# One y tile per x tile, a reordered whitening chain, packing by TensorE in pairs, and a reordered start in a convolution and whitening kernel

## The chip, the cores and the metric

The kernel runs on one core of one Trainium2 chip. Its engines are named as in the profile: PE (TensorE, with PEld for its weight loads), DVE (VectorE), ACT (ScalarE), POOL (GpSimd) and SP (SyncE, which only issues DMAs). The metric is the device time of one execution in microseconds; lower is better.

## The reference

Two layers, all in float32. Layer 0 is a separable long convolution of x (4 images, 64 channels, 256 x 256) with a filter that a small network of sines computes; layer 1 whitens the 64 channels. Cut to what matters:

```python
# layer 0, for each filter (X: rows, Y: columns)
h = sin(freq * (z @ w1 + b1)); h = sin(freq * (h @ w2 + b2)); h = sin(freq * (h @ w3 + b3))
h = (h @ wo) * exp(-t * abs(deltas))             # 256 taps for each channel
k[c] = outer(hx[:, c], hy[:, c])
y = irfft2(rfft2(x) * rfft2(k) / 512)[:256, :256]  # causal 2-D convolution
x = y + x * bias[:, None, None]
# layer 1
x1 = transpose(x, (1, 0, 2, 3)).reshape(64, -1)
x1_s = x1[:, ::9]                                 # every 9th pixel
xc = x1 - mean(x1_s)
cov = x1_s @ x1_s.T / n + 0.01 * eye(64)
normA = norm(cov); Y = cov / normA; Z = eye(64)
for _ in range(5):                                # Newton-Schulz
    T = 0.5 * (3 * I - Z @ Y); Y = Y @ T; Z = T @ Z
out = (Z / sqrt(normA)) @ xc
```

## The kernel before, in words

The kernel has four parts in time.

*The start* (lines 85 to 175). The filter network's weights (`zw`, `cols`, `wbd`, `decay`) and two tables (`mask`, `bias`) are loaded, five of the six on ACT's queue; three layers of product, Identity, range reduction on DVE and Sin give `taps`, which go to HBM (`g_d`) and come back as Toeplitz tiles, each row shifted by one. `busy` issues products of zeros as filler for TensorE between the layers. A float32 product is issued as two passes, so `busy(8)` shows as 16 matmuls.

*The convolution.* There are 32 steps, each one image `n` and one block `g` of 8 channels; each step is worked off in four groups of two channels (`c` = 0, 2, 4, 6). In `group`, TensorE multiplies one pair by the first filter (`job1`, from the x tile) and, interleaved with it, the pair of two groups earlier by the second filter (`job2`). ACT copies the first result to `o1`; DVE adds `x * bias` to the second result and writes y (line 398). `store` sends y to HBM, to `y_d`. The first two groups and the last two run alone, in `half_group`. Once a step's y is whole, `pack_ops` adds nine `copy_predicated` on DVE that pick every 9th pixel into `samp`; `pack` runs about three of them in each group. For the last half of the last step the picking is done by TensorE (`pack_by_pe`, one product for each of nine phases and two halves with the matrices `pick`). `covariance(n)` multiplies the samples of an image once its last step is done.

*The chain* (lines 473 to 562). From the covariance follow the norm, five Newton-Schulz iterations of small 64 x 64 products, the scaled matrix `W` and the vector `shift`.

*The whitening.* y is read back in 32 pieces of 2 MB (`load_y`), multiplied by `W` (line 580), shifted on ACT and DVE (lines 585 and 588) in place, and written out by DMAs that GpSimd issues (line 593).

In memory, the pool `big` holds two x tiles (`in`) and two y tiles (`out`). After the convolution, x, y, filter, sample and two extra tiles become homes for pieces of y: `homes` lists 13, in the order in which they are taken, and piece 13 takes the first home again after its store. The order of work is written out by hand and kept on every engine (`manual_schedule`): SyncE issues x loads, y stores, filter loads (`blocks`) and reads of y in program order, and a DMA that waits holds up those behind it. `early` says after which step and group how many pieces of y are already asked for; the rest of the 13 follow after the last covariance. SyncE's DMAs use eight completion semaphores in turn, so each also waits for the eighth before it.

Of the kernel before, what the change touches and what calls it, by code (L numbers as in the profile page):

```python
# [48 lines left out]
CG = 8  # L49
# [16 lines left out]
def conv_whiten_kernel(ctx: ExitStack, tc: tile.TileContext, a: dict, out: bass.AP):  # L66
# [4 lines left out]
    big = ctx.enter_context(tc.tile_pool(name="big", bufs=2))  # L71
# [13 lines left out]
    scratch = big.tile([P, 16, L], F32, tag="out", name="scratch")  # L85
# [4 lines left out]
    nc.scalar.dma_start(out=cols, in_=a["cols"])  # L90
    wbd = scratch[:, 0:2, :].rearrange("p a w -> p (a w)")[:, 0 : 3 * P]
    nc.scalar.dma_start(out=wbd, in_=a["wbd"])
    decay = scratch[:, 15, :]
    nc.scalar.dma_start(out=decay, in_=a["decay"])
    mask = const.tile([P, NB, H2, STEP], I32, tag="mask", name="mask")
    nc.scalar.dma_start(out=mask, in_=a["mask"])
    bias = const.tile([P, C], F32, tag="bias", name="bias")
    nc.scalar.dma_start(out=bias, in_=a["bias"].partition_broadcast(P))
# [11 lines left out]
    x_tiles = [big.tile([P, CG, H2, L], F32, tag="in", name=f"x{u}") for u in range(2)]  # L110
    for c in range(0, CG, 2):
        load_x(x_tiles[0], *steps[0], c)

# [22 lines left out]
    bf = const.tile([P, 3], F32, tag="bf", name="bf")  # L136

    nc.vector.memset(bf[:, 0:1], 0.0)
    nc.scalar.activation(bf[:, 1:2], bf[:, 0:1], AF.Sin)
# [12 lines left out]
    for i in range(3):  # L152
        for u in range(2):
            pm = psA.tile([P, P], F32, tag="psA", name=f"pm{i}_{u}")
            nc.tensor.matmul(pm, lhsT=wt, rhs=hs[u], start=True, stop=True)  # L155
            half = slice(u * P, (u + 1) * P)
            arg, k, nxt = (scratch[:, 2 + 3 * i + v, half] for v in range(3))
            nc.scalar.activation(arg, pm, AF.Identity, bias=bf[:, i : i + 1], scale=freq)
            nc.vector.tensor_scalar(k, arg, 1.0 / (2.0 * math.pi), MAGIC, ALU.mult, ALU.add)
            nc.vector.tensor_scalar(k, k, MAGIC, None, ALU.subtract)  # L160
            for part in (TP1, TP2):
                nc.vector.scalar_tensor_tensor(arg, k, -part, arg, ALU.mult, ALU.add)  # L162
            nc.vector.tensor_scalar(arg, arg, 3.1415925, -3.1415925, ALU.min, ALU.max)
            nc.scalar.activation(nxt, arg, AF.Sin)
            hs[u] = nxt
        wt = wbd[:, i * P : (i + 1) * P]
        busy((8, 10, 9)[i])
# [92 lines left out]
    def half_group(item, which):  # L260

        g, n, c, xt, yt, o1s = item
# [11 lines left out]
        for m in range(H2):  # L274
            for u in range(2):
                ps = jobs[u][0][m]
                if which == 0:
                    copy = nc.vector.tensor_copy if u else nc.scalar.copy
                    for to, fr in ((slice(0, HP), slice(HP, P)), (slice(HP, P), slice(0, HP))):
                        copy(o1s[u][to, m], ps[fr])  # L280
                else:
                    ch = g * CG + c + u
                    nc.vector.scalar_tensor_tensor(  # L283
                        yt[:, c + u, m], xt[:, c + u, m], bias[:, ch : ch + 1], ps,
                        ALU.mult, ALU.add,
                    )

    def pack_by_pe(g, n, yt, cs):
# [15 lines left out]
        nc.vector.tensor_copy(dst[:, 1], pk[:, 1].rearrange("p c j -> p j c"))  # L304
# [15 lines left out]
    def covariance(n):  # L320
# [20 lines left out]
        {"t": (tpool, "toep"), "s": (spool, "samp"), "i": (big, "in"), "o": (big, "out"), "e": (epool, "extra")}[k]  # L341
        for k in "eetssitsoiots"
# [28 lines left out]
    early = {(26, 4): 1, (26, 6): 1, (27, 4): 1, (28, 2): 1, (29, 6): 1, (31, 4): 2, (31, 6): 1}  # L371
# [8 lines left out]
    def group(first, second):  # L380

        units = []
        g1, n1, c1, x1, _, o1s1 = first
        g2, n2, c2, x2, y2, o1s2 = second
# [7 lines left out]
        for u in range(2):  # L392
            o1 = o1pool.tile([P, H2, L], F32, tag="o1", name=f"o1_{g1}_{n1}_{c1 + u}")
            for to, fr in ((slice(0, HP), slice(HP, P)), (slice(HP, P), slice(0, HP))):
                nc.scalar.copy(o1[to], units[u][0][0][fr])  # L395
            o1s1.append(o1)
            ch = g2 * CG + c2 + u
            nc.vector.scalar_tensor_tensor(  # L398
                y2[:, c2 + u], x2[:, c2 + u], bias[:, ch : ch + 1], units[u][1][0],
                ALU.mult, ALU.add,  # L400
            )
# [4 lines left out]
    def store(second):  # L406
        g, n, c, _, yt, _ = second
# [7 lines left out]
        if last and c == CG // 2 - 2 or not last and c == CG - 2:  # L415
            todo.extend(pack_ops(g, n, yt, slice(0, c + 2)))

    engines = mybir.EngineType
    with tc.manual_schedule(
# [9 lines left out]
        for i, (g, n) in enumerate(steps):  # L429
            xt = x_tiles[i % 2]  # L430
            yt = big.tile([P, CG, H2, L], F32, tag="out", name=f"y_{g}_{n}")
            for c in range(0, CG, 2):
                item = (g, n, c, xt, yt, [])
# [7 lines left out]
                if i == 0 and c == 6:  # L441
# [3 lines left out]
                    twice = const.tile([C, 2, C], F32, tag="twice", name="twice")  # L445
                    for u in range(2):
                        nc.vector.tensor_copy(twice[:, u], ident[0:C, 0:C])

                j, cj = i - (c < 4), (c - 4) % CG
                if 0 <= j < len(steps) - 2:  # L450
                    load_x(x_tiles[j % 2], *steps[j + 2], cj)
# [8 lines left out]
        g, n, c, xt, yt, _ = pending[0]  # L460
# [6 lines left out]
        pack_by_pe(g, n, yt, slice(CG // 2, CG))  # L467
# [3 lines left out]


    spare = {}
    for i in range(2):
        t = o1pool.tile([P, H2 * L], F32, tag="o1", name=f"chain{i}")
        for j in range(5):
            spare[5 * i + j] = t[0:C, 72 * j + 72 : 72 * j + 72 + C]
    ones = spare[9]
    nc.gpsimd.memset(ones, 1.0)  # L479
    i15 = spare[8]  # L480
    nc.vector.tensor_scalar(i15, ident[0:C, 0:C], 1.5, None, ALU.mult)
    spots = {"A": [0], "sq": [1], "Y": [2, 3], "T": [4, 5], "Z": [6, 7], "Zs": [1]}

    columns = [t[0:C, 440 + k : 441 + k] for k in range(H2 * L - 440)]

    def column():
        return columns.pop()

    def matrix(tag):
        spots[tag].append(spots[tag].pop(0))  # L490
        return spare[spots[tag][-1]]

    def product(lhsT, rhs, name):
        p = psA.tile([lhsT.shape[1], rhs.shape[1]], F32, tag="psA", name=name)
        nc.tensor.matmul(p, lhsT=lhsT, rhs=rhs, start=True, stop=True)  # L495
        return p

    def keep(p, name, tag):
        t = matrix(tag)
        nc.vector.tensor_copy(t, p)  # L500
        return t


    pd = product(fold, cov, "pd")
    A = matrix("A")
    nc.vector.scalar_tensor_tensor(A, ident[0:C, 0:C], EPS, pd[:, 0:C], ALU.mult, ALU.add)
    mean = column()
    nc.scalar.copy(mean, pd[:, C : C + 1])

    def root(v, name):  # L510

        s0 = column()
        nc.scalar.activation(s0, v, AF.Sqrt)  # L513
        r = column()
        nc.vector.reciprocal(r, s0)
        s1 = column()
        nc.vector.scalar_tensor_tensor(s1, v, r, s0, ALU.mult, ALU.add)
        s2 = column()
        nc.vector.tensor_scalar(s2, s1, 0.5, None, ALU.mult)
        return s2  # L520

    sq = matrix("sq")
    nc.vector.tensor_tensor(sq, A, A, ALU.mult)
    rowsum = column()
    nc.vector.tensor_reduce(rowsum, sq, AX.X, ALU.add)
    ssq = column()
    nc.vector.tensor_copy(ssq, product(ones, rowsum, "pn"))
    norm = root(ssq, "norm")
    rnorm = column()
    nc.vector.reciprocal(rnorm, norm)  # L530

    Y = matrix("Y")
    nc.vector.tensor_scalar(Y, A, rnorm, None, ALU.mult)
    Z = None
    for it in range(N_ITER):
        ZY = Y if Z is None else product(Z, Y, f"ZY{it}")
        T = matrix("T")
        nc.vector.scalar_tensor_tensor(T, ZY, -0.5, i15, ALU.mult, ALU.add)
        if it < N_ITER - 1:
            nextY = product(Y, T, f"YT{it}")  # L540
        if Z is None:
            newZ = T
        else:
            newZ = matrix("Z")
            nc.scalar.copy(newZ, product(T, Z, f"TZ{it}"))
        if it < N_ITER - 1:
            Y = keep(nextY, f"Y{it + 1}", "Y")
        else:
            snorm = root(norm, "snorm")
            rsnorm = column()  # L550
            nc.vector.reciprocal(rsnorm, snorm)
        Z = newZ

    Zs = matrix("Zs")
    nc.vector.tensor_scalar(Zs, Z, rsnorm, None, ALU.mult)
    twice = twice.rearrange("p u c -> p (u c)")
    W = o1pool.tile([P, H2 * L], F32, tag="o1", name="W")[:, 0:C]
    nc.vector.tensor_copy(W, product(twice, Zs, "pw"))
    shift0 = column()
    nc.vector.tensor_scalar(shift0, product(Zs, mean, "pz"), -1.0, None, ALU.mult)  # L560
    shift = const.tile([P, 1], F32, tag="shift", name="shift")
    nc.vector.tensor_copy(shift, product(twice, shift0, "ps"))
# [91 lines left out]
```

## Time and profile before

| | us |
|---|---|
| median of 3 runs (lowest, highest) | 917.46 (916.84, 920.22) |
| the profiled execution, its own time | 916.79 |
| span of the profiled execution, first to last instruction | 914.9 |
| PE busy (share of the span) | 789.4 (86%) |
| DVE busy | 657.7 (72%) |
| ACT busy | 479.1 (52%) |
| first convolution matmul | 19.63 |
| end of the last Toeplitz product | 621.4 |
| first store of the result issued | 653.81 |

Times inside the profile count from the start of the span. Shares of busy time are averages over stages that have different limits. The granted clock of TensorE was 0.946 on average. `yi` are pieces of y read back, `y_d` is y in HBM, `ph` and `p` are results of Toeplitz products, `pk` of packing, `pc` of the covariance, `po` of the whitening.

### The profile page before, as it was taken

How to read it: one execution, taken by the hardware profiler on the slowest of the kernel's cores; microseconds unless marked ns; L12 is line 12 of the kernel's file. 1: busy time of each engine (PE TensorE's matmuls, PEld its weight loads, DVE VectorE, ACT ScalarE, POOL GpSimd, SP SyncE). 2: the span in 40 equal slices, each digit the busy share in tenths (PEclk: the TensorE clock that was granted, in tenths of full speed). 3: DMA queues.
4: the chain of work that ended last, by engine and by line, in shares of the span. 5: the costliest groups of instructions: out<-in, count | busy, mean ns of one | idle time of the engine just before them, and what ended most of it. 6: DMA issues, size and time to landing. Idle time of an engine off the chain costs nothing.

```text
span 914.9 us, 28251 instructions
## 1 busy us (share of the span) xinstructions
PE 789.4 (86%) x11876; PEld 633.3 (69%) x11876; DVE 657.7 (72%) x882; ACT 479.1 (52%) x791; POOL 31.8 (3%) x71
## 2 busy tenths in 40 slices
PE   8999999999999999999999999997877777765500
PEld 7999999999999999999999999996311111121100
DVE  3468776878687868786878666866699999986500
ACT  2545454545454545454545444540598888865400
POOL 3000000000000000000000000000110000000010
PEclk9999999999999999999999999998799999987655
DMA  4988788788788888888997897849999999999998
GB/s 155 295 264 262 247 262 265 232 269 260 249 263 262 248 256 264 258 253 275 285 275 227 310 378 289 300 139 406 422 418 426 428 429 429 430 430 427 433 433 333
DMA packets 117549, 285.59 MB, mean 312 GB/s; under 512 B 8973, under 2 KB 91312, under 8 KB 109744
## 3 DMA queue, kind: packets, MB, share of 16 engines
q1 hardware_dynamic: 110224, 216.09, 69.2%
q0 software_dynamic: 6336, 67.11, 17.3%
q8 instruction: 94, 1.54, 0.7%
q10 hardware_dynamic: 864, 0.60, 0.2%
q14 instruction: 31, 0.25, 0.1%
HBM read 149.35 MB, written 134.42 MB: 310 GB/s over the span
## 4 chain that ended last, share of the span: by engine, by line
PE 68%; issue 15%; DVE 14%; ACT 0%; DMA 0%; POOL 0%; POOLq 0%; DVEq 0%; ACTq 0%; SPq 0%
PE p L214 63%; DVE yi L588 12%; PE pc L326 2%; PE ph L246 1%; PE pk L294 1%; POOL out_dram L593 0%; DMA toep<-g_d 0%; DVE y L283 0%; PE busy L149 0%; PE po L580 0%; PE ZY L495 0%; PE YT L495 0%; PE pm L155 0%; DVE scratch L162 0%; ACT L513 0%
## 5 line engine op out<-in xcount | busy, mean ns | idle before, releaser
L214 PE MATMUL p<-toep,o 64*64 64x64 f32 (+3 forms) x5040 | 578.4, 284 | 0.0
L214 PE MATMUL p<-toep,x 64*64 64x64 f32 (+3 forms) x5040 | 578.3, 284 | 0.0
L214 PEld LDWEIGHTS p<-toep,x 64*128 64x128 f32 (+1 forms) x5040 | 534.2, 166 | 23.1
L214 PEld LDWEIGHTS p<-toep,o 64*128 64x128 f32 (+1 forms) x5040 | 535.4, 166 | 10.5 <-issue 0.2
L395 ACT COPY o<-p 64x512 f32<-64x512 f32 x504 | 292.4, 580 | 297.3 <-PE p L214 289.7
L312 DVE COPY_PREDICATED samp<-mask,y 128x448 f32<-128x448 int32 (+3 forms) x288 | 281.1, 976 | 6.6
L398 DVE SCALAR_TENSOR_TENSOR y<-x,bias,p 128x512 f32<-128x512 f32 x252 | 177.3, 744 | 138.4 <-PE p L214 130.2
L588 DVE TENSOR_SCALAR yi<-po,shift 64x512 f32<-64x512 f32 x256 | 192.1, 750 | 24.5 <-PE po L580 18.2
L580 PE MATMUL po<-yi,W 64*64 64x512 f32 x1024 | 153.2, 674 | 61.8 <-DVE yi L588 40.4
L585 ACT ACTIVATE yi<-po,shift 64x512 f32<-64x512 f32 x256 | 174.9, 683 | 43.7 <-PE po L580 36.7
L580 PEld LDWEIGHTS po<-yi,W 64*64 64x64 f32 x1024 | 36.8, 146 | 176.9 <-DVE yi L588 125.0
L593 POOL DMA_DIRECT2D out_dram<-yi x44 | 23.7, 538 | 263.5 <-DVE yi L588 100.6
L479 POOL MEMSET chain<- 64x64 f32 x1 | 0.1, 145 | 602.2 <-PE ph L246 602.2
L326 PEld LDWEIGHTS pc<-samp 128*64 128x64 f32 x464 | 14.4, 137 | 2.0 <-issue 1.2
L326 PE MATMUL pc<-samp 128*64 128x65 f32 x464 | 15.1, 223 | 0.5 <-ACT samp L303 0.4
L149 PE MATMUL busy<-idle 128*128 128x128 f32 x94 | 12.9, 301 | 0.0
L149 PEld LDWEIGHTS busy<-idle 128*128 128x128 f32 x94 | 12.4, 216 | 0.2 <-issue 0.2
L280 DVE COPY o<-ph 64x256 f32<-64x256 f32 x8 | 3.4, 422 | 9.1 <-PE ph L246 8.9
L294 PE MATMUL pk<-y,pick 128*128 128x112 f32 (+1 forms) x36 | 7.7, 389 | 2.5 <-DVE y L283 2.5
L334 DVE SCALAR_TENSOR_TENSOR cov<-pc,cov 128x65 f32<-128x65 f32 x4 | 0.9, 227 | 12.4 <-PE pc L326 12.4
L294 PEld LDWEIGHTS pk<-y,pick 128*128 128x128 f32 x36 | 7.2, 260 | 2.8 <-issue 2.7
L280 ACT COPY o<-ph 64x256 f32<-64x256 f32 x8 | 2.9, 367 | 10.0 <-DMA toep<-g_d 8.5
(81 smaller groups left out, 79.7 us busy)
## 6 DMA issues: line engine op xcount, KB each, us to landing
x<-in_x_dram SPq DMA_DIRECT2D x128, 512.0 KB, 5.3
y_d<-y SPq DMA_DIRECT2D x256, 256.0 KB, 3.5
yi<-y_d SPq DMA_DIRECT2D x32, 2048.0 KB, 15.7
out_dram<-yi POOLq DMA_DIRECT2D x28, 2048.0 KB, 44.6
out_dram<-yi POOLq DMA_DIRECT2D x16, 512.0 KB, 9.0
toep<-g_d SPq DMA_DIRECT2D x29, 256.0 KB, 6.2
toep<-g_d SPq DMA_DIRECT2D x29, 192.0 KB, 5.6
toep<-g_d SPq DMA_DIRECT2D x6, 128.0 KB, 3.1
```

The lines of the kernel that those rows point to most:

```text
L149: nc.tensor.matmul(p, lhsT=idle[:, 0:P], rhs=idle[:, P : 2 * P], start=True, stop=True)
L214: mm = nc.tensor.matmul(ps[q : q + w, m, HP * k : L], lhsT=src[parts, k // 2, m * P + q : m * P + q + w], rhs=t[parts, : stop : -1] if k e ...
L246: mm = nc.tensor.matmul(ps[m][:, HP * k : L], lhsT=src[parts, k // 2, m * P : (m + 1) * P], rhs=t[parts, : stop : -1] if k else t[parts, : ...
L294: nc.tensor.matmul(pk[:, b, :, 0:nj], lhsT=pick[:, (s - b) % STEP, :], rhs=yt[:, cs, b, s : s + STEP * (nj - 1) + 1 : STEP], start=(s == 0 ...
L312: nc.vector.copy_predicated(dst, m, src)
L326: nc.tensor.matmul(pc[half], lhsT=samp[n][:, b, j, 0:C], rhs=samp[n][:, b, j, :], start=(b == 0 and j < 2), stop=(b == H2 - 1 and j >= NJ ...
L395: nc.scalar.copy(o1[to], units[u][0][0][fr])
L398: nc.vector.scalar_tensor_tensor(y2[:, c2 + u], x2[:, c2 + u], bias[:, ch : ch + 1], units[u][1][0], ALU.mult, ALU.add,)
L580: nc.tensor.matmul(po[u][halves[k]], lhsT=W[halves[u]], rhs=yt[halves[u], cols[k]], start=True, stop=True,)
L585: nc.scalar.activation(yt[halves[0], cols[k]], po[0][halves[k]], AF.Identity, bias=shift[halves[k]])
L588: nc.vector.tensor_scalar(yt[halves[1], cols[k]], po[1][halves[k]], shift[halves[k]], None, ALU.add)
L593: nc.gpsimd.dma_start(out=o[:, end - part : end], in_=yt[:, end - part : end])
```

## The change

The convolution writes y into the x tile. The pools `in` and `out` of two tiles each become one pool of four x tiles; step i+2 is loaded into the tile of step i-2, at the same `c`. The filter network's scratch moves to an extra tile. `homes` and `early` change with it: of the first 13 pieces nine instead of eight are asked for inside the steps, pieces 5 and 6 in step 30 and step 31 at `c` = 2.

At the start, ACT issues one DMA (`cols`) and then runs the first Sin; `wbd`, `decay`, `mask` and `bias` go to SyncE's queue, between and behind the first x loads. The first filler is 5 products instead of 8. An activation with Sqrt runs in step 0.

`pack_by_pe` is called twice, for two channels each; in the first call ACT makes both copies. The chain becomes a function, `whitening`, inside the manual schedule: the first iterate is a polynomial of the covariance and its square and cube, which are multiplied while the norm is still computed; afterwards T is squared and M is multiplied by it (three rounds), the mean is carried as a 65th column of Z, the last T is written twice side by side so that one product gives `W` and `shift` for both halves, and the scaling comes last. `spin` issues products of the identity as filler.

```diff
-    big = ctx.enter_context(tc.tile_pool(name="big", bufs=2))
+    xpool = ctx.enter_context(tc.tile_pool(name="xpool", bufs=4))
...
-    scratch = big.tile([P, 16, L], F32, tag="out", name="scratch")
+    scratch = epool.tile([P, 16, L], F32, tag="extra", name="scratch")
...
     nc.scalar.dma_start(out=cols, in_=a["cols"])
+    bf = const.tile([P, 3], F32, tag="bf", name="bf")
+    nc.vector.memset(bf[:, 0:1], 0.0)
+    nc.scalar.activation(bf[:, 1:2], bf[:, 0:1], AF.Sin)
...
-    nc.scalar.dma_start(out=wbd, in_=a["wbd"])
+    nc.sync.dma_start(out=wbd, in_=a["wbd"])
...
     for c in range(0, CG, 2):
         load_x(x_tiles[0], *steps[0], c)
+        if c == 0:
+            nc.sync.dma_start(out=decay, in_=a["decay"])
+    nc.sync.dma_start(out=mask, in_=a["mask"])
+    nc.sync.dma_start(out=bias, in_=a["bias"].partition_broadcast(P))
...
-        busy((8, 10, 9)[i])
+        busy((5, 10, 9)[i])
...
-        nc.vector.tensor_copy(dst[:, 1], pk[:, 1].rearrange("p c j -> p j c"))
+        copy = nc.vector.tensor_copy if cs.stop == CG else nc.scalar.copy
+        copy(dst[:, 1], pk[:, 1].rearrange("p c j -> p j c"))
...
-        for k in "eetssitsoiots"
+        for k in "eetssiistiits"
...
-    early = {(26, 4): 1, (26, 6): 1, (27, 4): 1, (28, 2): 1, (29, 6): 1, (31, 4): 2, (31, 6): 1}
+    early = {
+        (26, 4): 1, (27, 0): 1, (27, 4): 1, (28, 0): 1, (29, 6): 1, (30, 2): 1, (31, 2): 1, (31, 4): 1, (31, 6): 1
+    }
...
-                y2[:, c2 + u], x2[:, c2 + u], bias[:, ch : ch + 1], units[u][1][0],
+                x2[:, c2 + u], x2[:, c2 + u], bias[:, ch : ch + 1], units[u][1][0],
...
-                j, cj = i - (c < 4), (c - 4) % CG
-                if 0 <= j < len(steps) - 2:
-                    load_x(x_tiles[j % 2], *steps[j + 2], cj)
+                    nc.scalar.activation(bf[:, 0:1], samp[0][:, 0, 0, C : C + 1], AF.Sqrt)
+                if i + 2 < len(steps):
+                    load_x(x_tiles[(i + 2) % 4], *steps[i + 2], c)
...
-        pack_by_pe(g, n, yt, slice(CG // 2, CG))
+        for lo in range(CG // 2, CG, 2):
+            pack_by_pe(g, n, yt, slice(lo, lo + 2))
         covariance(NB - 1)
         while len(loaded) < len(homes):
             load_next()
+        W, shift = whitening(i15, ones)
```

The new chain, with its filler (a placed tile is a piece of an `o1` buffer; `product` is as before):

```python
def spin(times):
    p = psA.tile([P, P], F32, tag="psA", name=f"spin{len(spins)}")
    for _ in range(times):
        nc.tensor.matmul(p, lhsT=ident, rhs=ident, start=True, stop=True)

def whitening(i15, ones):
    pd = product(fold, cov, "pd")
    nc.vector.scalar_tensor_tensor(A, ident[0:C, 0:C], EPS, pd[:, 0:C], ALU.mult, ALU.add)
    nc.vector.tensor_tensor(sq, A, A, ALU.mult)
    pa2 = product(A, A, "pa2")
    pn = product(ones, sq, "pn")
    ...
    nc.vector.tensor_reduce(ssq, pn, AX.X, ALU.add)
    nc.scalar.activation(s0, ssq, AF.Sqrt)
    ...
    pa3 = product(A2a, A, "pa3")
    spin(7)
    ...
    nc.vector.scalar_tensor_tensor(rn, r3, hm, h, ALU.mult, ALU.add)
    ...
    nc.vector.scalar_tensor_tensor(U, pa3, rn_c, A2b, ALU.mult, ALU.add)
    nc.vector.scalar_tensor_tensor(V, U, rn_c, A1b, ALU.mult, ALU.add)
    nc.vector.scalar_tensor_tensor(T, V, rn_c, one_i15, ALU.mult, ALU.add)
    nc.vector.tensor_scalar(M, V, rn_c, -2.0, ALU.mult, ALU.mult)
    ...
    for k in range(1, N_ITER - 1):
        pq = product(T, T, f"pq{k}")
        if before is not None:
            next_z(k - 1, before)
        spin(1)
        nc.vector.tensor_copy(Q, pq)
        pm = product(Q, M, f"pm_{k}")
        ...
    pw = product(T, Z, "pw")
    nc.vector.tensor_scalar(W, pw[:, 0:C], rs, None, ALU.mult)
    nc.scalar.activation(shift, pw[:, C : C + 1], AF.Copy, scale=nrs)
```

## The prediction

> **What bounds the kernel now.** I read the slices first: which engine is full in which stage.
>
> ```profile
> PE   8999999999999999999999999997877777765500
> DMA  4988788788788888888997897849999999999998
> GB/s 155 295 264 262 247 262 265 232 269 260 249 263 262 248 256 264 258 253 275 285 275 227 310 378 289 300 139 406 422 418 426 428 429 429 430 430 427 433 433 333
> ```
>
> A slice is 22.9 us. TensorE is full for 26 slices (the convolution); from the 28th on the DMA engines are, at 406 to 433 GB/s (whitening: y is read back, transformed, written out). Between them lies the 27th slice, at 139 GB/s. So I cut the turn finer, with the table of windows (busy time of PE, PEld, DVE, ACT, POOL, then granted clock, DMA share, GB/s):
>
> ```profile
> 600.00:606.00 6.00, 6.00 (x142) 5.47 (x138) 3.15 (x4) 2.33 (x5) 0.00 (x0) 1.00 0.50 168
> 606.00:610.00 4.00, 4.00 (x48) 3.72 (x48) 0.23 (x1) 0.00 (x0) 0.00 (x0) 1.00 0.02 4
> 610.00:613.00 3.00, 3.00 (x94) 2.92 (x94) 2.43 (x4) 2.31 (x4) 0.00 (x0) 1.00 0.07 21
> 620.00:650.00 30.00, 20.14 (x205) 17.07 (x206) 15.97 (x47) 2.94 (x9) 0.00 (x0) 0.75 1.02 412
> 775.00:905.00 130.00, 58.98 (x360) 16.24 (x358) 72.46 (x97) 62.87 (x92) 9.66 (x19) 0.72 1.01 429
> ```
>
> The DMA engines are nearly idle until 613 and full from there to the end, through the serial chain too (620 to 650). The end is therefore set by two things: when TensorE's stream lets y come free, and how many bytes are still to be moved at 613. Who asks for them is SyncE's timeline:
>
> ```profile
> 577.39 0.40 SPq L350 DMA_DIRECT2D yi<-y_d  x1
> ...
> 613.33 0.94 SPq L350 DMA_DIRECT2D yi<-y_d  x2
> ...
> 617.25 0.42 SPq L350 DMA_DIRECT2D yi<-y_d  x1
> ...
> 627.21 11.32 SPq L350 DMA_DIRECT2D yi<-y_d  x5
> ```
>
> Tile 4 of y is read back at 577; tiles 5 and 6 only at 613, tile 7 at 617, 8 to 12 from 627. Thirteen tiles have a home before a store frees one.
>
> **The start.** From the timeline:
>
> ```profile
> 2.62 0.73 ACTq L98 DMA_DIRECT2D bias<-in_bias_dram  x1
> 3.38 1.28 ACT L139 ACT_TABLE_LOAD   x1 [3.38 <-issue]
> 3.73 3.70 PE L149 MATMUL busy<-idle 128*128 128x128 f32 x16
> 5.23 0.81 ACT L158 ACTIVATE scratch<-pm,bf,cols 128x128 f32<-128x128 f32 x2 [0.35 <-issue]
> 7.61 0.95 PE L155 MATMUL pm<-scratch 128*128 128x128 f32 x4 [0.19 <-ACT scratch L164]
> 19.63 6.41 PE L246 MATMUL ph<-toep,x 64*128 64x256 f32 x64 [0.32 <-DMA toep<-g_d]
> ```
>
> ACT issues five DMAs before it loads Sin's table at 3.38, and everything up to the first convolution matmul (19.63) hangs on the chain behind it. With one DMA ahead (0.74 to 1.14) the load ends at about 2.45, bf follows when cols lands (0.74 + 2.0 us), and the first Identity waits for pm, about 3.3 instead of 5.23: 1.9 us. The filler of layer 1 becomes 5 products, 10 passes: 3.70/16 = 0.231 us each, from 3.73 to 6.04. Layer 2's product would be ready at 7.61 - 1.9 = 5.7 and waits for that filler: 1.6 us remain. Layer 2's filler keeps its 20 passes, which took 2.40 us (0.12 each) from 8.40. [...] The granted clock column says 1.00 here, but passes of 0.231 and then 0.12 us show two speeds. By the row, those passes start at 6.8 mostly fast and cost 0.2; [...]. I take **-1.4**, between -1.9 and +0.6. SyncE now issues wbd (second), decay (after one x piece), mask and bias (after all x). wbd, 4.7 us to land before, is ahead of x now and needed at 5.7; decay is needed at 13; mask moves from 9.5 to about 10.5, pick's 5.7 us on GpSimd then end at 16.5, before the fences wanted at 18.5. SyncE's next work, the taps' store, is at 13.8: covered.
>
> **The convolution.** y goes into x's place; the same 252 additions of 744 ns. The x load of step i+2 comes up to two groups earlier, but its first piece now waits for the last copy_predicated of step i-2 (976 ns each, three after the group's two additions: 4.5 us after the matmuls end). Behind it on SyncE stand a filter load and the next y stores, wanted 6 us after the same instant: nothing late. The piece is wanted seven groups of 4.6 us later and lands in 5.3. **0**, as TensorE has no idle time in line 214's rows. Sqrt's table load, moved to step 0, takes 1.28 us of the 2.2 that ScalarE is idle in each group; [...]. The trace shows none behind line 513's load (ends 638.14, activation at 638.16): 0.
>
> **The turn.** `early` now asks for tile 5 in step 30 (c = 2, about 585), tile 6 in step 31 (c = 2, about 604.6), 7 at 613, 8 at 617. Their homes are free: x tiles of steps 28 and 29 were last read by packing a step earlier. So two tiles of 2.1 MB move while the DMA engines were idle. One costs 4.9 us (stores at the end follow each other at 4.86; a load and a store take 9.8): **-9.8**. Left at 613: tiles 7 to 12 and 2.1 MB of y, 7 x 4.9 = 34.3 us. Tile 9 waits for step 30's last packing (625.0), in time; tile 10 for packing of step 31 (about 631.2), with some 2 us to the first byte, when the queue is dry at about 633 (613.8 + 4 x 4.9): the two meet, and I allow **+0.8**. All thirteen are in at about 649.
>
> **Chain and packing by PE.** Its length counts only if the stores come after 649.
>
> ```profile
> 624.08 6.87 DVE L312 COPY_PREDICATED samp<-mask,y 128x448 f32<-128x448 int32 x10
> 631.99 3.71 PE L326 MATMUL pc<-samp 128*64 128x65 f32 x116 [0.41 <-ACT samp L303]
> 636.86 1.28 ACT L513 ACT_TABLE_LOAD   x1
> 649.55 15.78 PE L580 MATMUL po<-yi,W 64*64 64x512 f32 x98
> 651.64 48.72 DVE L588 TENSOR_SCALAR yi<-po,shift 64x512 f32<-64x512 f32 x63 [1.81 <-PE po L580]
> 653.81 0.73 POOL L593 DMA_DIRECT2D out_dram<-yi  x1 [35.49 <-PE po L580]
> ```
>
> Pairs: 72 passes instead of 36. Between 72 x 0.107 (the half of 7.67/36 each) and 72 x 0.116 (weights of 128 columns, as the filler's), starting at 621.4 rather than 623.9: done by 629.1 to 629.8, yet the covariance also needs VectorE's copies, which run without a gap to 630.95. So it starts at 631.0: -1.0. Chain: from the covariance's end to the first po was 13.8 us, with rounds of 1.75 (ZY at 640.60, 642.36, 644.12). Now: 4.0 us to the first T (no table load, root and reciprocal in one, three VectorE steps of 0.28 instead of two), three rounds of two products and two VectorE steps (0.64 a pair at full clock, 0.78 at half) plus 0.15 for z and spin: 4.4; pw and W 0.7. Sum 9.1: -4.7. The 8 spins keep the clock: the first eight po took 1.99, later ones 1.09: -1.0. First store at 653.8 - 6.7 = 647.1; if the spins run slow (14 passes, 3.2 us instead of 1.6), some 649. The first stores then flow alone, four quarters at 1.55 us of which 1.22 are moved, until tile 13 is asked for: **+1.5**.
>
> Sum: 914.9 - 1.4 + 0 - 9.8 + 0.8 + 1.5 = 906.0 span. Around the span lie 1.9 us (916.79 - 914.9), so 907.9 for the profiled execution, which stood 0.7 under the median of 917.46: **908.5**.
>
> **The rivals.**
> - *No gap at all*: start -1.9, no dry queue, 903.2 + 2.6 = 905.8. For: before, the queue never ran dry after 613. Against: homes now wait for packing.
> - *The stores become the bound*: the chain is short by only 1 us, as the spins stand in TensorE's order ahead of each product. First store 652.8; DMA dry from 649 to 654.8: +5.8, 914.4. For: granted clock 0.5 in the old chain. Against: they start while it is 1.
> - *The early reads don't come early*: the lanes behind SyncE's queue hold tiles 5 and 6 until 613. Then only the start counts: 916.1. Against: nothing large is queued at 585 or 604.
> - *Slower*: x's first piece waits too long for packing. Place: SyncE at c = 0 of each step; slack 32 us less 4.5 and the landing. It decides from a landing of about 27 us; the price is the excess in 30 steps, and 0.45 us a step is already +0.5% over the median. At 0.9 a step: 935. For: reads of y landed up to 25.4 us after issue. Against: those are in the whitening.
>
> **How the numbers follow.** Forecast 0.66, no gap 0.10, stores the bound 0.12, reads not early 0.07, slower 0.05. The forecast's unknowns (start -1.9 to +0.6, gaps 0 to 4) give 905.8 to 912; with a part of the third case the range is 904.5 to 913.5. A measurement tells about 0.5%, 4.6 us. Faster: 0.66 + 0.10 and half of 0.12, 0.82; same: the other half and 0.07, 0.13; slower 0.05.
>
> **What would show it.** Reads of tiles 5 and 6 at about 584 and 603; first convolution matmul at 18.2; windows from 590 to 612 at 300 GB/s or more; first store near 645.7; DMA share about 1 in 612 to 905. It is wrong if TensorE shows idle time in the convolution, if the share falls under 0.9 between 630 and 660, or if the first store comes after 650.

## The result, and the profile after

The changed kernel takes 910.47 us, the median of four runs (910.07 to 911.4), against 917.15 for the kernel before (four runs). The ratio is 0.9921, with an interval from 0.9905 to 0.9937: 0.8% faster, and 2.0 us more than the 908.5 that was predicted. The profiled execution took 911.4 us. Its span is 909.6 us; 1.8 us lie around it. The span of before was 914.9, so between these two executions the change took **5.3 us** out of it, where the prediction had 8.9. The profiled execution is the slowest of the four: the spans of the other three were 908.2 to 908.6, at a mean granted clock of 0.955 to 0.963 instead of 0.951, and no trace of them was kept.

The slices of the changed kernel's page (22.7 us each) show the part that worked. The 27th slice has 253 GB/s instead of 139; the 29th has 346 instead of 422.

```profile
PE   8999999999999999999999999999977777775500
DMA  4998788797888788878987898879899999999998
GB/s 154 303 305 261 250 243 263 251 276 247 253 262 265 247 255 267 263 249 253 297 282 234 285 400 323 290 253 386 346 383 433 428 432 429 428 433 428 432 430 342
```

SyncE's timeline of the changed kernel says why: pieces 5 and 6 of y are asked for at 585 and 603, instead of both at 613.

```profile
576.53 0.41 SPq L352 DMA_DIRECT2D yi<-y_d  x1
585.05 0.47 SPq L352 DMA_DIRECT2D yi<-y_d  x1
603.36 0.44 SPq L352 DMA_DIRECT2D yi<-y_d  x1
612.60 0.43 SPq L352 DMA_DIRECT2D yi<-y_d  x1
```

The windows of the changed kernel (busy time of PE, PEld, DVE, ACT and POOL; then granted clock, DMA share and GB/s) show the turn cut finer:

```profile
600.00:606.00 6.00, 6.00 (x140) 5.42 (x138) 2.55 (x4) 2.32 (x4) 0.00 (x0) 1.00 0.63 189
606.00:610.00 4.00, 4.00 (x92) 3.77 (x92) 0.23 (x1) 0.14 (x1) 0.00 (x0) 1.00 0.99 401
610.00:613.00 3.00, 3.00 (x66) 2.91 (x58) 2.97 (x4) 2.18 (x4) 0.00 (x0) 1.00 0.42 147
613.00:648.00 35.00, 31.49 (x332) 27.85 (x332) 22.54 (x58) 4.84 (x18) 0.20 (x1) 0.88 1.02 401
630.00:636.00 6.00, 5.14 (x94) 5.14 (x96) 0.64 (x4) 0.45 (x3) 0.00 (x0) 0.50 1.01 428
648.00:652.00 4.00, 4.00 (x32) 1.21 (x28) 3.17 (x5) 3.09 (x5) 0.73 (x1) 0.76 0.27 111
652.00:660.00 8.00, 8.00 (x53) 2.17 (x48) 7.76 (x11) 7.80 (x12) 2.66 (x5) 1.00 0.83 336
680.00:905.00 225.00, 124.13 (x838) 28.47 (x830) 161.77 (x216) 144.42 (x212) 18.11 (x34) 0.84 1.01 429
```

From 606 to 610 the DMA engines now move 401 GB/s, where it was 4. But from 648 to 652 their share is 0.27, and 0.83 from 652 to 660; before, they were full there. The thirteen pieces are in, every home is taken, and the next read can only follow a store. The timeline of the changed kernel at the turn shows that store coming late:

```profile
620.55 8.28 PE L295 MATMUL pk<-x,pick 128*128 128x58 f32 x72
623.39 6.87 DVE L314 COPY_PREDICATED samp<-mask,x 128x448 f32<-128x448 int32 x10
630.86 6.20 PE L328 MATMUL pc<-samp 128*64 128x65 f32 x116 [2.04 <-ACT samp L304]
646.59 13.66 PE L616 MATMUL po<-yi,chain 64*64 64x512 f32 x85 [0.38 <-DVE chain L537]
650.90 0.73 POOL L629 DMA_DIRECT2D out_dram<-yi  x1 [30.45 <-DVE yi L624]
```

The covariance (`pc`) takes 6.20 us where it took 3.71, with the same 116 matmuls: TensorE had been idle for 2.04 us before it, and the window from 630 to 636 has a granted clock of 0.50. The first store goes out at 650.90, not at the forecast 645.7.

At the start, the timeline of the changed kernel has:

```profile
1.16 1.28 ACT L94 ACT_TABLE_LOAD   x1 [1.16 <-PEq L675]
3.42 0.89 ACT L159 ACTIVATE scratch<-pm,bf,cols 128x128 f32<-128x128 f32 x2 [0.77 <-PE pm L156]
3.74 2.50 PE L150 MATMUL busy<-idle 128*128 128x128 f32 x10
6.89 3.05 PE L150 MATMUL busy<-idle 128*128 128x128 f32 x20
18.51 0.67 PE L247 MATMUL ph<-toep,x 64*128 64x256 f32 x2 [0.42 <-DMA toep<-g_d]
19.44 5.83 PE L247 MATMUL ph<-toep,x 64*128 64x192 f32 x62 [0.26 <-DMA toep<-g_d]
```

The first Identity runs at 3.42 instead of 5.23. Of these 1.8 us only 1.1 reach the first convolution matmul (18.51 instead of 19.63), mainly because the second layer's 20 filler passes take 3.05 us instead of 2.40. In the trace's own record of the granted clock, full speed comes at 8.24 us here, in the middle of these passes (they start 0.21 us apart before it and 0.11 after it), and in the kernel before at 7.22, ahead of them (8.40). And only 0.8 reach the stream behind it: its third matmul waits for another part of the filter until 19.44.

### The profile page after: what moved, and what is told of

Read it like the earlier page. It is cut to its first block, busy times and chain, and to the rows that moved or that the text cites. A ratio compares the mean times of both kernels' runs of the same rounds, so it can differ in the third digit from the quotient of the medians.

```text
span 909.6 us, 28286 instructions
## 1 busy us (share of the span) xinstructions
PE 792.2 (87%) x11928; PEld 636.7 (70%) x11928; DVE 657.6 (72%) x882; ACT 479.8 (53%) x798; POOL 31.4 (3%) x71
## 4 chain that ended last, share of the span: by engine, by line
PE 68%; DVE 15%; issue 14%; DMA 1%; POOL 0%; ACT 0%; POOLq 0%; SPq 0%; DVEq 0%; ACTq 0%
PE p L215 64%; DVE yi L624 13%; PE pc L328 2%; PE ph L247 1%; DVE samp L314 1%; PE busy L150 1%; POOL out_dram L629 0%; PE po L616 0%; DMA toep<-g_d 0%; DVE x L284 0%; PE spin L429 0%; PE pm L156 0%; DMA scratch<-in_zw_dram 0%; DMA g_d<-scratch 0%; DVE scratch L163 0%
## 5 line engine op out<-in xcount | busy, mean ns | idle before, releaser
L314 DVE COPY_PREDICATED samp<-mask,x 128x448 f32<-128x448 int32 (+3 forms) x288 | 281.0, 976 | 6.7
L402 DVE SCALAR_TENSOR_TENSOR x<-x,bias,p 128x512 f32<-128x512 f32 x252 | 177.3, 743 | 138.9 <-PE p L215 138.5
L616 PE MATMUL po<-yi,chain 64*64 64x512 f32 x1024 | 152.7, 668 | 59.9 <-DVE yi L624 41.7
L616 PEld LDWEIGHTS po<-yi,chain 64*64 64x64 f32 x1024 | 35.9, 145 | 175.7 <-DVE yi L624 129.6
L328 PE MATMUL pc<-samp 128*64 128x65 f32 x464 | 17.3, 243 | 2.0 <-ACT samp L304 2.0
L328 PEld LDWEIGHTS pc<-samp 128*64 128x64 f32 x464 | 16.8, 155 | 3.2 <-ACT samp L304 2.2
L295 PE MATMUL pk<-x,pick 128*128 128x56 f32 (+1 forms) x72 | 8.3, 292 | 0.0
L295 PEld LDWEIGHTS pk<-x,pick 128*128 128x128 f32 x72 | 8.1, 192 | 0.1
```

The source lines that it names most:

```text
L295: nc.tensor.matmul(pk[:, b, :, 0:nj], lhsT=pick[:, (s - b) % STEP, :], rhs=yt[:, cs, b, s : s + STEP * (nj - 1) + 1 : STEP], start=(s == 0 ...
L314: nc.vector.copy_predicated(dst, m, src)
L328: nc.tensor.matmul(pc[half], lhsT=samp[n][:, b, j, 0:C], rhs=samp[n][:, b, j, :], start=(b == 0 and j < 2), stop=(b == H2 - 1 and j >= NJ ...
L402: nc.vector.scalar_tensor_tensor(x2[:, c2 + u], x2[:, c2 + u], bias[:, ch : ch + 1], units[u][1][0], ALU.mult, ALU.add,)
L616: nc.tensor.matmul(po[u][halves[k]], lhsT=W[halves[u]], rhs=yt[halves[u], cols[k]], start=True, stop=True,)
```

## The experiments

The question was which of three things sets the end now: the bytes that are left at 613, the moment of the first store, or the stores' own rate; and what made the first store late. Each ratio is to the kernel before on the same chip, with its interval.

**The early reads taken back.** Everything else stays as in the changed kernel.

```diff
-  ... (29, 6): 1, (30, 2): 1, (31, 2): 1, (31, 4): 1, (31, 6): 1
+  ... (29, 6): 1, (31, 4): 2, (31, 6): 1
```

> The changed kernel, with pieces 5 and 6 of y asked for in step 31 at c = 4, as before the change (one edit in early). Theory A (the end is set by the bytes left at 612.6, less what the DMA engines stand idle after): two pieces more, 9.8 us, of which about 4.5 fill the idle stretch from 648 to 672; 915 to 916.5 us, and no stretch without DMA near 650. Rival B (the end is set by the first store alone): no change, 910 to 911. Rival C (the gain is all in the start and the chain): no change.

916.76 us, ratio 0.9987 (0.998 to 0.9994): with all the rest of the change, only 1.2 us is left of the gain, close to what theory A said (915 to 916.5). Its windows:

```profile
606.00:613.00 7.00, 7.00 (x141) 6.57 (x141) 2.50 (x4) 2.12 (x4) 0.00 (x0) 1.00 0.02 5
648.00:652.00 4.00, 4.00 (x32) 1.19 (x28) 2.44 (x4) 2.43 (x4) 0.34 (x1) 0.68 0.99 418
```

The hole is back ahead of 613, and the one at 648 is gone. The first store went out at 651.66, 2.15 us earlier than in the kernel before, and the span is 914.6 against 914.9: here the bytes set the end, and an earlier store is worth nothing.

**The old start in the changed kernel, and the new start in the old one.** In the first, ACT issues the five DMAs again ahead of Sin's table and layer 1 gets its 8 products back; the second is the kernel before with the new start alone.

```diff
-    nc.scalar.activation(bf[:, 1:2], bf[:, 0:1], AF.Sin)
...
-    nc.sync.dma_start(out=wbd, in_=a["wbd"])
+    nc.scalar.dma_start(out=wbd, in_=a["wbd"])
+    nc.scalar.dma_start(out=decay, in_=a["decay"])
+    nc.scalar.dma_start(out=mask, in_=a["mask"])
+    nc.scalar.dma_start(out=bias, in_=a["bias"].partition_broadcast(P))
...
+    nc.scalar.activation(bf[:, 1:2], bf[:, 0:1], AF.Sin)
...
-        busy((5, 10, 9)[i])
+        busy((8, 10, 9)[i])
```

> The changed kernel with the start of before: five DMAs on ScalarE ahead of Sin's table, 8 products of filler in layer 1. Theory A: the convolution starts 0.8 later (26.04 instead of 25.26) and all behind it moves with it: 911.3, +0.8. Rival (the start is covered by later waits): 910.5, no change.

> The kernel before with the new start alone: table of Sin ahead, weights on SyncE, five products of filler in layer 1; tiles, reads, packing and chain as before. Theory A (the start moves the convolution by 0.2 to 1.2 us by how long TensorE's first filler stays slow, and all after it by as much): time 0.2 to 1.2 us below before, 916.1 to 917.1. Rival B (the start is worth the 2.7 us by which the kernel without it stood above the changed one): 914.3 to 915.2.

The first took 913.03 us, ratio 0.9951 (0.9939 to 0.9963), some 2.7 us above the changed kernel by the ratios: more than expected. The second took 915.76, ratio 0.9988 (0.9979 to 0.9997): 1.1 us below before, between 0.3 and 1.9. So the start is worth about 1 us alone (in its timeline the convolution's stream begins 0.7 us earlier than before, at 25.08 instead of 25.78), and rival B (2.7 us) is out for it. Why its removal cost more in the changed kernel is not settled. The first kernel's profiled execution took 912.1, the least of its five, at a mean granted clock of 0.963, where the other four had 0.951 to 0.955, and does not show it. What that timeline does show is the covariance:

```profile
633.43 3.71 PE L328 MATMUL pc<-samp 128*64 128x65 f32 x116 [2.02 <-ACT samp L304]
```

Here is the same idle time of 2.02 us ahead of the covariance, and yet 3.71 us at full clock. Of six profiled kernels with this gap, five had a slow covariance (6.20, 6.07, 6.37, 6.20 and 5.28 us) and this one did not.

**Filler ahead of the covariance.** Eight products between the packing and the covariance.

```diff
         for lo in range(CG // 2, CG, 2):
             pack_by_pe(g, n, yt, slice(lo, lo + 2))
+        spin(8)
         covariance(NB - 1)
```

> The changed kernel with 8 products of the identity (16 passes, 1.9 us) between packing and covariance, so that TensorE isn't idle there. Theory A (TensorE's clock falls to half in the 2 us of waiting, the covariance takes 6.2 instead of 3.7, and the first store sets the end): covariance 3.7, first store at 648.4 instead of 650.9, time 908 to 909. Rival B (bytes alone): first store earlier, time 910.5. Rival D (the clock falls all the same): covariance 6.2, no change.

909.59 us, ratio 0.9911 (0.9898 to 0.9923): by the ratios 0.9 us below the changed kernel, within the intervals, and short of theory A's 908 to 909. Its timeline:

```profile
628.27 1.99 PE L429 MATMUL spin<-ident 128*128 128x128 f32 x16
630.47 3.71 PE L328 MATMUL pc<-samp 128*64 128x65 f32 x116 [0.21 <-ACT samp L304]
644.75 15.73 PE L617 MATMUL po<-yi,chain 64*64 64x512 f32 x97 [0.38 <-DVE chain L537]
649.06 0.73 POOL L630 DMA_DIRECT2D out_dram<-yi  x1 [28.99 <-DVE yi L625]
```

The idle time filled, the covariance is back at 3.71, and so it is in the three later kernels with the same filler: the half clock came with the wait (2.04 us in the changed kernel, 0.21 here), not with what the covariance computes. The first store came 1.84 us earlier than in the changed kernel (0.4 of it because this execution reached the covariance earlier) and the span was 1.7 us shorter, although the clock now fell to 0.5 within the chain (642 to 648): 10.25 us from `pd` to the first `po`, not 9.21.

**Packing at once, as before.**

```diff
-        for lo in range(CG // 2, CG, 2):
-            pack_by_pe(g, n, yt, slice(lo, lo + 2))
+        pack_by_pe(g, n, yt, slice(CG // 2, CG))
```

> The changed kernel with one packing of four channels instead of two pairs. Theory A (clock): TensorE is idle before packing instead of after it; the covariance starts at 630.9 to 631.3 but takes 3.7 to 4.5: first store 1.5 to 2.3 earlier, 908.7 to 909.5. Rival (the pairs save what they were made for): covariance 0.5 to 1 later, 911 to 911.5.

911.2 us, ratio 0.9928 (0.9915 to 0.9941), not to be told from the changed kernel; theory A's 908.7 to 909.5 was missed, and the time alone fits the rival. Its timeline shows theory A's mechanism all the same:

```profile
624.60 7.91 PE L295 MATMUL pk<-x,pick 128*128 128x116 f32 x36 [2.56 <-DVE x L284]
632.91 3.71 PE L328 MATMUL pc<-samp 128*64 128x65 f32 x116 [0.40 <-ACT samp L304]
649.56 0.73 POOL L628 DMA_DIRECT2D out_dram<-yi  x1 [27.69 <-DVE yi L623]
```

Now TensorE waits 2.56 us ahead of the packing, and the clock falls there (0.50 from 624.08 to 630.91). The packing hardly depends on it: in the kernel before, which packs in the same way (36 passes in 7.67 us, 7.91 here), they start 0.21 us apart at half clock and 0.20 after 628.44, and VectorE's copies beside it, which end at 631.63, hide all but 0.9 us of it. The covariance and the chain run at full clock: 16.65 us from the covariance's start to the first store, 20.04 in the changed kernel. The span, 908.2, is 1.4 us shorter with it, though this execution came to its covariance 2.05 us later (632.91): 0.6 for the packing, the rest from its start and its convolution. These are single executions, however, here the second fastest of five and in the changed kernel the slowest of four; the medians show no gain. The pairs did not remove the wait. They moved it from ahead of work that hardly depends on the clock to ahead of work that does (the covariance, 3.71 us at full clock here and 6.20 in the changed kernel).

**The old chain in the changed kernel.** The Newton steps of before in the place of `whitening`.

```diff
-        W, shift = whitening(i15, ones)
+    spots = {"A": [0], "sq": [1], "Y": [2, 3], "T": [4, 5], "Z": [6, 7], "Zs": [1]}
...
+    pd = product(fold, cov, "pd")
+    A = matrix("A")
...
```

> The changed kernel with the chain of before (five Newton-Schulz rounds, no filler; Sqrt's table stays loaded in step 0). Theory A (once all thirteen pieces are in, about 649, the end moves with the first store): first store some 3.5 to 4.5 later than 650.9, the DMA engines stand still until about 656; 913.5 to 915. Rival B (bytes alone): 910.5, no change.

914.87 us, ratio 0.9973 (0.9963 to 0.9984): 4.8 us lost by the ratios (0.9973 less 0.9921, of 917), as theory A said. The first store of the old chain, and its windows:

```profile
655.41 0.73 POOL L717 DMA_DIRECT2D out_dram<-yi  x1 [37.32 <-DVE yi L712]
```

```profile
648.00:652.00 4.00, 2.82 (x13) 1.87 (x16) 1.00 (x5) 0.21 (x1) 0.00 (x0) 0.50 0.33 139
652.00:660.00 8.00, 8.00 (x64) 2.48 (x56) 6.57 (x9) 6.56 (x10) 1.84 (x4) 0.86 0.36 147
```

The first store comes 4.5 us later than in the changed kernel, and the DMA engines stand mostly still from 648 to 656.

**One more early read.** Piece 7 is asked for together with piece 6.

```diff
-  (31, 2): 1, (31, 4): 1,
+  (31, 2): 2,
```

> The changed kernel with piece 7 of y asked for in step 31 at c = 2, right behind piece 6, instead of at c = 4; its home (the samples of image 2) is free at 605. The reads then end about 1.5 to 2 us earlier. Theory A (first store sets the end): no gain, 910 to 911, only a longer idle stretch before the first store. Rival B (bytes at 612 set the end): 908.5 to 909.

910.93 us, ratio 0.9929 (0.9916 to 0.9943): nothing gained. Its windows:

```profile
606.00:613.00 7.00, 7.00 (x142) 6.66 (x142) 3.67 (x5) 2.32 (x4) 0.00 (x0) 1.00 1.09 448
648.00:652.00 4.00, 4.00 (x36) 1.15 (x32) 3.72 (x5) 3.63 (x6) 0.92 (x2) 0.82 0.11 46
```

The hole ahead of 613 is now full, and what was moved there is missing from 648 to 652 (0.11 instead of 0.27). A byte moved earlier buys nothing once the homes are full and the first store is late. Rival B, the bytes, is out.

**Less filler at the start.** 5 products instead of 10 in layer 2.

```diff
-        busy((5, 10, 9)[i])
+        busy((5, 5, 9)[i])
```

> The changed kernel with 5 instead of 10 products of filler in layer 2. Over the runs so far these 20 passes took 2.40, 3.05, 3.31 and 3.72 us, as TensorE reached full speed at another moment in each, and layer 3 waited for them. Theory A: with 10 passes (2.3 at half speed) layer 3 never waits; first convolution matmul at 18.0 to 18.3 in each run, time 0.3 to 1.0 lower, 909.5 to 910.2. Rival (filler too short, the clock is late for layer 3 and its filler): first convolution matmul later than 18.5, time 910.5 or more.

910.32 us, ratio 0.992 (0.9904 to 0.9935): no gain that can be told. The convolution's stream did begin 1.2 us earlier than in the changed kernel's profile (23.84 against 25.01), but by the third covariance, at 601.76, nothing was left of it (601.49).

**The tiles and the early reads alone.** The kernel before with y in x's place and the early reads; start, packing and chain as before.

```diff
-    big = ctx.enter_context(tc.tile_pool(name="big", bufs=2))
+    xpool = ctx.enter_context(tc.tile_pool(name="xpool", bufs=4))
...
-    early = {(26, 4): 1, (26, 6): 1, (27, 4): 1, (28, 2): 1, (29, 6): 1, (31, 4): 2, (31, 6): 1}
+        (26, 4): 1, (27, 0): 1, (27, 4): 1, (28, 0): 1, (29, 6): 1, (30, 2): 1, (31, 2): 1, (31, 4): 1, (31, 6): 1
```

> The kernel before with one part of the change alone: four x tiles with y in place of x, homes and early as changed; start, packing and chain as before. Theory A: two pieces fewer left at 613, but the first store stays at about 653.8 while the reads are all in at 649: about 5 of 9.8 us are kept, 912.5 to 914. Rival B (bytes alone): 908. Rival C (the tiles don't matter): 917.

915.16 us, ratio 0.998 (0.9973 to 0.9986): under 2 us of the 9.8 that the two pieces are worth in bytes, and less than theory A expected (912.5 to 914). The profiled execution, at 916.92, stood 1.8 us above that median. Its first store, at 655.96, is 2.2 us later than in the kernel before: it came to its third covariance 2.0 us later (604.27). With a store as early as before's (653.81), the table below would put its span at 912.9, 2.0 us under before's, and that is about what the median shows: the store sets the end. So neither half of the change gains much alone: the tiles and the reads without the rest 0.2%, all the rest without the reads 0.13%, together 0.79%.

**Covers for the clock.** First the eight products ahead of the covariance and two products instead of one in each filler place of the chain; then also the first store as two halves; then also the 5 products in layer 2 and piece 7 with piece 6, by the edits shown for these.

```diff
+        spin(8)
...
-            spin(1)
+            spin(2)
...
+                if i == 0 and w == 0:
+                    nc.gpsimd.dma_start(out=o[:, cols[k]], in_=yt[:, cols[k]])
```

> Eight passes of filler between the packing and the last covariance (which alone gave 909.6), and two passes instead of one in each of the chain's six filler places. Theory A (the end follows the first store, and the half clock from 642 to 648 comes from too thin work on TensorE): with the clock full through the chain, first output products at 644.2 (0.5 us less than 644.75) and first store at 647.6 to 648.2 instead of 649.06; time 908.6 to 909.4. Rival B (six passes of 0.23 us lie on the chain, whose rounds have 0.3 us or less of TensorE idle): rounds of 1.6 to 1.7 us instead of 1.46, first store 649 to 650.5, time 909.5 to 911.

> As the kernel with both covers, and the first store goes out as two of 512 columns, each after its own half of the eviction. Theory A (the end follows the first store): first store about 0.8 us earlier (one eviction of 0.78 us less ahead of it), time 0.4 to 0.8 us below the kernel with both covers. Rival B (two stores of 2 KB rows are slower or the queue's issue of 0.73 us each takes it back): time the same to 0.3 us above.

> Both covers, the first store in two halves, five passes of filler less in layer 2, and the seventh early read at the same place as the sixth. Theory A (with the first store 2 to 3 us earlier than in the changed kernel, the end is still set by it): first store 646.5 to 648, time 907.5 to 909, the least of all kernels here. Rival B (the reads, which end at 648 to 650, or the stores' own rate set the end from there on, so nothing more is gained): no less than the 909.6 of the kernel with the eight passes alone.

910.21 us (ratio 0.992, 0.9907 to 0.9932), 909.86 (0.992, 0.9906 to 0.9934) and 908.77 (0.9907, 0.9891 to 0.9922). In the first, the clock is 1.00 in every window from 622 to 672, and the first products take 3.43 us to the first store instead of 4.31. But the filler lies on the chain, whose rounds take 1.9 us instead of 1.46. From `pd` to the first `po` it is 10.38 us, so both theories had half of it, and against the changed kernel the two halves nearly cancel (13.81 us from `pd` to the first store, 13.52 there). In the second, the first store follows 2.66 us after the first `po`, 0.8 earlier as expected, yet it carries half the bytes, and nothing measurable is gained. The third has the earliest first store of all kernels and the lowest time:

```profile
629.98 3.71 PE L328 MATMUL pc<-samp 128*64 128x65 f32 x116 [0.20 <-ACT samp L304]
644.39 13.53 PE L617 MATMUL po<-yi,chain 64*64 64x512 f32 x90 [0.38 <-DVE chain L537]
647.03 1.29 POOL L629 DMA_DIRECT2D out_dram<-yi  x2 [27.44 <-ACT yi L622]
```

Its lead over the changed kernel, 1.3 us by the ratios, lies within the intervals.

**All of them together.** The first store and the span of each profiled execution (`pd` is the first product of the chain):

| kernel | covariance, us | `pd` to first `po` | first store | span | span less first store |
|---|---|---|---|---|---|
| before | 3.71 | 13.53 | 653.81 | 914.9 | 261.1 |
| new start alone | 3.71 | 13.53 | 653.53 | 914.2 | 260.7 |
| reads late | 6.07 | 9.20 | 651.66 | 914.6 | 262.9 |
| tiles and reads alone | 3.71 | 13.39 | 655.96 | 915.1 | 259.1 |
| old chain | 6.37 | 13.08 | 655.41 | 913.7 | 258.3 |
| changed | 6.20 | 9.21 | 650.90 | 909.6 | 258.7 |
| less filler | 5.28 | 9.70 | 650.73 | 910.1 | 259.4 |
| covers in the chain | 3.71 | 10.38 | 650.37 | 909.1 | 258.7 |
| piece 7 earlier | 6.20 | 9.19 | 650.35 | 909.3 | 259.0 |
| and first store in halves | 3.71 | 10.38 | 650.28 | 910.1 | 259.8 |
| old start | 3.71 | 9.20 | 650.08 | 910.3 | 260.2 |
| packing at once | 3.71 | 9.20 | 649.56 | 908.2 | 258.6 |
| filler ahead of covariance | 3.71 | 10.25 | 649.06 | 907.9 | 258.8 |
| all covers | 3.71 | 10.37 | 647.03 | 906.7 | 259.7 |

In the eleven kernels with the early reads the first store moves over 9 us, and the span less the first store stays between 258.3 and 260.2 us. (In the two kernels with halves the first store carries half the bytes, which puts them about 1 us higher.) With late reads it is larger, and in the reads-late kernel an earlier store shortens nothing. Part of this is only a common shift, as a convolution that ends late moves reads and stores alike. Counted from the third covariance, the first store of the eleven still moves from 46.0 to 53.4 us, and the end from 305.3 to 311.7; the reads-late kernel, with its first store at 49.2, ends at 312.2, where the changed one (49.4) ends at 308.1. At the early end the gain stops: the old-start kernel (46.0) ends at 306.2, no sooner than the three between 46.4 and 46.7 (305.3 to 306.2), and its DMA share from 650 to 652 is 0.93, so that its reads and its first store nearly meet. What follows the first store goes at the same rate as before: 429 GB/s at a full share of the DMA engines, from 680 to 905 in the changed kernel and from 775 to 905 in the kernel before. That is the answer to the question: the end is the later of two dates, the bytes' and the first store's plus about 259 us.

## Why the prediction was right or wrong

The sign was right, and 910.5 lies within the range; the forecast mechanism carries the gain. Yet two of the marks by which it was to be known wrong came up: a DMA share under 0.9 between 630 and 660, and a first store after 650. The stretch from 590 to 612 moved 248 GB/s (before 124), not 300 or more. By its steps, in the profiled execution:

- **The turn, -9.8: right in its dates.** The reads went out at 585.05 and 603.36 (forecast about 585 and 604.6). All thirteen pieces were in at about 649, as forecast. Of the 9.8 us in bytes about 6 show in the time: that is what taking the reads back cost.
- **Convolution, 0: right.** From the stream's first matmul to the third covariance it is 576.48 us in both profiles. The table load took 1.28 us, the activation behind it followed within 0.02 us, and nothing waited for it.
- **The start, -1.4: half of it.** The stream began 0.77 us earlier. The forecast took the 20 passes of layer 2 as mostly fast, a cost of 0.2; the +0.6 at the other end of its range was an estimate, all 20 at the slow 0.231 us a pass. With the new start they took between 2.40 and 3.72 us in nine profiled kernels: 2.40 in the kernel with filler ahead of the covariance, 3.05 in the changed kernel, where full speed came at 8.24, and 3.72 with packing at once. With the old start they took 2.40 in three out of three; in the kernel before full speed came at 7.22, ahead of them (8.40). So the forecast's mostly fast passes were one end of the spread, and what sets the value that an execution meets was not shown.
- **The covariance's start, -1.0: -0.36** (630.86 and the 0.77 of the start, against 631.99). VectorE's last copies ended at 630.26, and the three copies of `pk` on ACT stand between them and the covariance: 0.60 us that the step left out.
- **The covariance itself, never counted: +2.5.** This is the largest error of the sum. The prediction saw that TensorE would be done with the packing at 629.1 to 629.8 and that the covariance could not start before 631, and did not price the idle time in between. A sign of it stood in the profile of before: TensorE waits 2.54 us ahead of the packing, and the granted clock is 0.50 from 625.03 to 628.44. The packing did not show the price, as its passes start 0.21 us apart at half clock and 0.20 from 628.44 on; the covariance's do depend on the clock (in the changed kernel they start 0.054 us apart on average at half clock and 0.029 after 636.29).

```profile
623.92 7.67 PE L294 MATMUL pk<-y,pick 128*128 128x116 f32 x36 [2.54 <-DVE y L283]
```

- **The chain, -4.7: -4.3.** From the covariance's end to the first `po` it was 9.53 us (forecast 9.1, before 13.85). The old chain put back cost 4.8 us.
- **The first products at full clock, -1.0: 0.** From the first `po` to the first store it took 4.31 us (before 4.26), at a clock that had fallen again at 646.5. In the two kernels that had the same chain and kept the clock (old start, packing at once) it took 3.42: the term would have been 0.8 there. Single fillers kept the clock in two profiled kernels of seven; double ones did in three of three, at their own price (rounds of 1.9 us instead of 1.46).
- **The gap at piece 10 and the stores alone, +2.3: in size too much, in place wrong.** The queue did not run dry at 633; all of the hole is at the first store.

The first store was thus late by 0.6 (start) + 0.6 (covariance's start) + 2.5 + 0.4 (chain) + 1.0 (first products) = 5.1 us, by the timeline 5.2 (650.9 against 645.7). By the table a store at 645.7 would mean a span of 904.4, if the bytes allowed it; the forecast of 906.0, with its 2.3 us for gaps, lay 1.6 above that, and so it missed by 3.6 us and not by 5.2. Whether the bytes would have allowed 904.4 no run shows. The rival "the stores become the bound" was right in its mechanism, a late first store with a dry queue from 649, and wrong in its cause: the spins did not stretch the chain, the covariance did. The prediction had said that the chain counts only if the stores come after 649, and put the first store 3.3 us ahead of that date. With the store 1.9 us behind it the chain's terms counted after all, and each further microsecond then had nearly its full price: the old chain put the first store 4.5 us later and the end 4.1.

## What to carry to other kernels

Where reads are bounded by the number of homes, work out two dates: when the last home is full, and when the first store leaves. Moving reads earlier pays until the two meet, and beyond that only an earlier store does. When a wait is shortened by splitting work, look at where TensorE's idle time goes: two idle microseconds ahead of a packing that is mostly covered and hardly depends on the clock (0.21 us a pass at half clock, 0.20 at full) cost little, ahead of the covariance they cost 2.5 us more through the clock in the profiled execution.

## What the runs showed of the hardware

- In the traces of the kernel before and of the changed kernel all changes of TensorE's granted clock lie whole multiples of 3.41 us apart (in the changed kernel at 8.24, 629.46, 636.29, 646.53 and 649.94, among others). The same holds, to about 0.03 us, for the changes that windows of 2 us show between 622 and 672 in eight more kernels; four kernels have none there. A change can fall in the middle of work: 636.29 lies within the covariance's matmuls. At the start, full speed came at 7.22 in the kernel before and at 8.24 in the changed kernel.
- The clock fell to 0.50 at an idle time of only 2.0 us in five profiled kernels of six, 0.3 to 2.0 us after the idle time had begun. Full speed came back 3.41 or 6.83 us later (634.55 to 637.20), in the middle of back-to-back matmuls; the covariance took 5.28 us where that was 634.55, and 6.20 in the changed kernel (636.29). In the sixth kernel (old start) the idle time was 2.02 us, and the clock stayed at 1.00 through it and through the covariance (3.71 us). What had to be idle for how long is therefore not settled.
- Not all matmuls here feel the clock alike. The packing's passes (128x116 from every 9th pixel) start 0.21 us apart at half clock and 0.20 at full, in the kernel before; the covariance takes 3.71 us at full clock and up to 6.37 with most of it at half.
- A stream of small products (64 by 64, with one filler product between them, rounds of 1.46 us) held the clock in some executions only. In five profiled kernels of seven it fell to 0.5, within the stream (641.6 in the one with filler ahead of the covariance) or at its end (646.5 in the changed one, 0.1 us ahead of the first `po`), and it stayed at 1.00 in the kernels with the old start and with packing at once. With two filler products in each place it stayed at 1.00 in all three.
- The convolution, with the same matmuls in the same order, took between 576.2 and 578.4 us from its stream's first matmul to the third covariance over the fourteen profiles; the granted clock was 1.00 from 26 to 600 in the kernel before and in the changed one. That is as much as several of the edits here are worth, and so a start that begins 1 us earlier is hard to see in the total.
